# Two graph layers on 64 graphs: tile places from a written table instead of rotating buffers, with the order of work written anew

## The chip, the cores and the metric

The kernel runs on one core of a Trainium2 chip. The core has five engines with a queue each: TensorE (PE, matrix products), VectorE (DVE), ScalarE (ACT), GpSimd (POOL) and SyncE (SP), which here issues all transfers between DRAM and the on-chip memory SBUF. PE writes its results to PSUM, eight banks of 2 KB in each of 128 partitions; DVE and ACT read them there. The metric is the device time in microseconds, the median of several runs.

## The reference

64 graphs of 256 nodes with 512 features go through two layers. All products are in float32.

```python
# x: (64, 256, 512); adj: (64, 256, 256), about 1.6% ones and the diagonal
h = relu(layernorm(x))                              # layer 0: gated attention, 8 heads of 64
q, k, v = h @ Wq.T, h @ Wk.T, h @ Wv.T
scores = where(adj != 0, q_h @ k_h.T / 8, -inf)     # per head, 256 x 256
c = concat_h(softmax(scores) @ v_h)
gate = sigmoid(concat(c, h) @ Wg.T + bg)
x = x + gate * h + (1 - gate) * c

h = relu(layernorm(x))                              # layer 1: GAT
Wh = h @ W                                          # 512 x 512
e = leaky_relu((Wh @ a1)[:, None] + (Wh @ a2)[None, :], 0.2)
att = softmax(where(adj == 0, -1e9, e))
x = x + elu(att @ Wh)
```

## The kernel before

**Tiling.** A graph's 256 tokens lie in two halves of 128 partitions (index `t`). The five large products (`qk`, `v`, `z` for the gate, `wh`, and `po` for the attention of layer 1) are done by a seven-product scheme for 2 x 2 block matrices instead of eight. `product` (lines 377 to 422) makes its steps: seven products on PE, named by a digit (`qk.1`, `v.6`, `wh.3`), which accumulate in three banks `pma`, `pmb`, `pmc`; and sums that empty the banks, `u1`, `u2`, `u3` into small tiles and `c00` to `c11` into the four quarters of the result. `u1` and `c00` are ACT copies (line 409), the others DVE additions (line 405). The sums of operand blocks that the scheme needs are made on POOL: `Sh`, `Sg`, `Sc`, `S1` (`token_sums`, line 375), `Sp` and `Rp` (lines 829 and 839). `wh.6`, for example, reads `S1.1`, which reads `S1.0`, which reads the transposed h of layer 1, `h1T`.

**Half-array work.** Two parts of layer 0 use only half of the PE array for one product. The scores (`sc.0` and `sc.1`, four heads each, line 589) have 64 rows of contraction: tile 64\*128. The weighing of v (`we.00` to `we.11`, line 649) gives 64 rows of output: tile 128\*64. All other products use the whole array, 128\*128.

**One graph's way.** Load x and adj (`load`, `edges`, `mask`); statistics and normalisation (`st0`, `root0`, `nb0`, `nm0`); a transpose by 32 x 32 blocks on DVE (`th`) and through DRAM (`sh` sends, `fh` fetches, four issues each); `qk`, `v`; scores. Then by head group and pair: `max` on DVE takes the masked row minimum of the negated scores out of PSUM and writes them into a tile `e` (line 599); `exp` on ACT with the row sums; `rec`; `scale` on POOL, for one pair on ACT; `turn`, `send`, `fetch` transpose it into `eT`; `we` multiplies with v into `pc`; `cT` copies that out on ACT, `tc`, `sc_c`, `fc` transpose it to c. `z` is the gate's product, followed by `tanh`, `diff`, `plus`, `mix`, `res`. Layer 1 is `st1` to `fh1`, `wh`, `ej` (the row of a2 products), `lo`, `lk`, `gm`, `gx`, `tg`, `sg`, `fg`, `po`, `neg`, `pos`, `xn`, `elu`, `add`, `store`.

**Order.** No scheduler decides the order. `PLAN` (line 23) gives every step of a graph a number; graph g's steps get 48 g added (`ROUND`), all steps of all graphs are sorted by the sum, and each engine's queue gets its steps in that order (lines 921 to 931). So in the middle of the run every 48 units the same sequence stands in each queue, one round, with steps of four or five graphs between each other: at 66 a graph g-1 is weighed where graph g, at 18, has its scores. The numbers are only sort keys; the time comes from the engines. `MOVED` has tables of their own for the first three and last three graphs, `ONCE` the loading of the weights and their sums.

**Memory.** `new` and `bank` (lines 273 to 277) hand out tiles. A pool has a number of buffers, and a new tile takes the place of an older one; the first write waits for the last reader of the tile that was there. There are 15 places of 4 KB for each partition in the pools S (3), qk (2), v, e (5), cT, z (2) and h, 8 places of 2 KB in tmp (5) and U (3), and one pool `ps` of eight banks. The pool e serves the `e`, the turned `eb` and the fetched `eT` tiles of all head pairs.

Of the kernel before, what the change touches and what calls it, by code (L numbers as in the profile page):

```python
# [8 lines left out]
F32 = mybir.dt.float32  # L9
# [14 lines left out]
load@-56.857 st0.0@-50.914 st0.1@-50.386 root0@-38.451 nb0@-30.73 nm0.1@-29.303 nm0.0@-26.84 th.1@-26.684  # L24
th.0@-25.569 sh@-25.308 fh@-18.664 edges@-17.435 Sh.0@-12.146 Sh.1@-9.433 qk.1@-2.883 qk.u1@-2.523 qk.6@-2.39
qk.u2@-2.35 Sh.2@-2.097 qk.7@-1.86 qk.2@-0.28 qk.5@0.348 qk.u3@2.467 Sh.3@2.69 qk.4@3.061 qk.c11@3.306 v.6@6.188
qk.c10@6.582 qk.3@8.941 v.1@10.525 qk.c01@12.52 qk.c00@13.266 v.5@13.583 mask@15.096 v.u1@16.001 v.u2@17.374
sc.0@18.765 v.7@18.861 max.001@19.626 max.000@19.866 v.u3@20.741 exp.001@21.355 max.010@22.095 exp.000@22.339
max.011@22.78 rec.00@22.853 v.c11@22.919 sc.1@23.918 v.3@24.165 scale.000@24.323 max.100@24.331 exp.011@24.947
v.c01@25.495 v.4@26.067 exp.010@27.66 max.110@28.028 max.111@28.261 exp.110@29.517 v.c10@29.519 rec.01@29.796  # L30
scale.001@29.819 scale.011@29.852 scale.010@32.212 turn.000@32.42 turn.001@32.926 exp.111@34.024 max.101@34.103
exp.100@34.466 rec.11@34.651 send.00@35.855 exp.101@36.261 scale.111@36.969 scale.110@37.232 turn.010@39.578
rec.10@42.242 turn.011@43.325 turn.110@43.328 turn.111@45.509 send.11@45.574 scale.100@45.966 scale.101@50.812
send.01@50.911 fetch.00@51.498 turn.101@52.285 Sg.0@52.35 fetch.11@54.685 fetch.01@54.883 turn.100@55.607
v.2@56.007 send.10@58.179 Sg.1@59.157 v.c00@61.854 fetch.10@64.798 we.00@69.417 we.01@69.42 we.11@69.423
we.10@69.426 Sg.3@69.567 Sg.2@69.717 cT.0@70.636 again.0@71.536 cT.1@71.646 Sc.0@75.856 tc.1@76.71 Sc.1@77.286
Sc.2@78.04 z.1@78.088 tc.0@78.815 z.6@79.585 Sc.3@80.277 z.u1@81.33 z.u2@83.091 z.5@83.343 sc_c@83.822
again.1@84.32 z.u2b@88.504 fc@88.967 z.7@89.255 z.u3@89.648 z.2@89.946 z.c11@89.956 z.4@91.345 z.c10@92.468
z.c00@92.495 z.3@93.65 z.c11b@93.91 z.c10b@94.31 tanh.11@94.446 diff.1@94.643 plus.1@94.689 diff.0@95.043
tanh.10@95.277 mix.1@95.529 z.c01@95.688 tanh.00@96.088 tanh.01@96.204 res.1@97.347 st1.1@97.913 mix.0@98.1  # L40
plus.0@98.329 res.0@98.674 st1.0@98.902 root1@100.345 nb1@101.327 nm1.1@102.323 nm1.0@102.364 th1.1@105.631
th1.0@105.724 sh1@112.437 fh1@116.746 wh.1@119.955 S1.2@121.277 S1.0@121.873 wh.u1@122.556 S1.1@123.554
wh.6@123.705 wh.u2@124.211 S1.3@125.364 wh.7@126.289 wh.5@126.586 wh.u3@126.939 wh.c11@128.246 wh.3@128.318
wh.2@129.72 wh.4@130.223 wh.c01@130.405 ej@130.423 Rp.0@130.663 wh.c00@130.978 wh.c10@131.603 lo.0@133.072
lo.1@133.143 lk@134.355 gm@135.48 gx.1@136.043 Rp.2@136.959 gx.0@137.014 tg@138.097 sg@139.813 fg@147.647
Rp.1@149.612 Sp.0@150.903 Sp.1@151.174 Sp.2@152.062 po.1@153.282 at.0@153.282 at.1@153.292 po.u1@153.578
po.6@154.2 gr@155.059 po.u2@155.153 po.7@155.525 po.5@157.176 po.2@157.832 Sp.3@159.316 po.u3@159.476
Rp.3@159.584 po.c11@159.831 po.4@160.018 po.c00@160.144 po.c10@160.279 po.3@160.606 po.c01@161.899 neg.0@162.539
pos.0@166.05 xn.0@166.37 neg.1@168.159 elu.0@168.402 pos.1@169.065 xn.1@169.357 elu.1@171.077 add.0@171.691
add.1@171.977 store.1@176.9 store.0@176.9  # L50
# [3 lines left out]
load@-84.838 st0.0@-70.024 st0.1@-65.46 nb0@-55.71 nm0.0@-52.129 nm0.1@-48.626 th.1@-27.17 Sh.0@-23.333  # L54
Sh.2@-18.64 qk.1@-18.134 qk.u1@-16.548 qk.5@-16.542 Sh.1@-16.358 qk.6@-13.56 qk.u2@-10.263 qk.2@-8.853
edges@-6.428 qk.7@-4.801 Sh.3@-2.103 qk.c00@-1.242 Sg.0@-1.138 Sg.2@-0.021 v.1@0.933 qk.u3@1.907 qk.c11@3.015
mask@3.359 qk.4@3.534 qk.c10@5.054 qk.3@7.14 sc.0@7.575 qk.c01@8.745 v.u1@9.235 max.001@9.244 v.6@9.543
exp.001@9.66 max.000@10.361 max.011@10.992 max.010@12.822 exp.000@13.344 Sg.1@13.537 v.u2@14.154 exp.011@14.257
rec.00@14.845 scale.001@17.841 exp.010@18.278 sc.1@18.944 max.101@19.34 max.100@19.638 v.7@19.923
scale.000@21.044 rec.01@21.889 max.110@22.998 exp.101@23.217 exp.100@23.47 v.5@23.574 exp.110@25.264  # L60
max.111@25.447 exp.111@25.812 turn.000@25.816 v.u3@26.697 turn.001@27.642 v.c11@29.899 scale.011@30.602
send.00@30.717 rec.10@32.367 v.4@33.611 scale.010@33.769 rec.11@36.532 v.2@36.903 turn.011@36.926
scale.111@37.258 turn.010@38.7 scale.110@39.488 v.c10@40.294 turn.111@42.261 turn.110@44.463 v.3@46.303
scale.100@46.341 send.01@46.819 again.0@51.194 turn.100@51.475 send.11@51.955 v.c01@52.024 scale.101@52.096
turn.101@52.671 fetch.00@54.339 send.10@57.895 Sg.3@58.891 fetch.01@61.895 fetch.11@62.369 v.c00@63.445
fetch.10@64.006 we.00@65.406 we.01@69.818 we.11@69.946 we.10@70.749 cT.0@71.689 Sc.2@73.405 cT.1@74.297
tc.0@74.313 tc.1@75.286 Sc.0@75.548 Sc.1@75.875 z.1@76.792 Sc.3@77.055 z.u1@78.295 z.6@83.257 sc_c@83.586
z.2@84.765 z.u2@85.297 z.u2b@85.717 z.5@86.726 fc@87.043 z.7@89.137 z.c00@89.679 z.u3@90.346 z.4@90.632
z.c11@91.163 z.3@91.422 z.c10@91.788 tanh.00@91.811 z.c11b@92.331 z.c10b@92.783 again.1@92.976 tanh.10@93.567
diff.1@93.819 z.c01@94.097 tanh.11@94.321 mix.1@94.45 plus.1@94.957 diff.0@95.286 plus.0@95.672 res.1@95.819  # L70
tanh.01@98.203 mix.0@98.476 st1.1@98.567 res.0@98.604 st1.0@100.036 root1@100.041 nb1@100.805 nm1.0@100.923
nm1.1@101.842 th1.0@102.876 th1.1@104.018 sh1@107.675 fh1@117.875 wh.1@120.728 S1.0@121.866 wh.5@121.891
S1.1@122.669 wh.u1@122.916 wh.6@123.053 wh.u2@123.088 S1.2@123.206 wh.2@123.428 wh.7@123.678 S1.3@124.231
wh.u3@124.694 wh.c11@126.668 wh.3@127.963 wh.c00@128.345 wh.c01@128.818 wh.4@129.098 Rp.0@129.804 ej@130.864
wh.c10@130.987 lo.0@131.977 lo.1@133.072 lk@133.478 gm@134.937 gx.1@135.784 gx.0@136.246 Rp.1@136.759 tg@137.074
sg@138.442 Rp.2@144.617 Rp.3@147.603 fg@148.992 Sp.0@149.583 Sp.2@150.994 Sp.1@151.262 po.1@153.424 gr@153.925
po.5@154.132 po.6@154.327 po.u1@155.598 po.u2@155.847 po.7@156.076 po.2@156.832 po.u3@156.928 po.c11@157.27
Sp.3@157.419 po.c00@158.191 po.4@158.939 po.3@159.535 po.c10@160.717 po.c01@160.77 neg.1@161.785 xn.1@162.021
pos.1@163.675 neg.0@165.715 elu.1@167.679 pos.0@168.736 xn.0@172.28 elu.0@173.244 add.1@175.909 add.0@175.952
store.1@177.279  # L80
""",
    1: """
load@-61.561 st0.0@-61.032 st0.1@-56.795 root0@-47.524 nb0@-45.124 nm0.0@-43.984 edges@-41.428 nm0.1@-41.37
mask@-39.285 th.1@-33.096 Sh.0@-25.932 qk.1@-24.669 Sh.1@-16.944 qk.5@-15.713 qk.6@-7.503 v.1@-4.955 Sh.3@-4.874
qk.u1@2.016 qk.u2@2.143 Sh.2@3.263 v.6@3.676 qk.7@5.202 qk.u3@8.896 qk.c11@8.906 v.5@9.315 qk.2@10.371
qk.3@11.942 qk.4@12.452 v.u1@14.127 qk.c01@15.444 qk.c00@15.51 v.u2@16.052 qk.c10@17.228 sc.0@17.921
max.000@18.683 max.001@19.555 exp.000@20.317 max.011@20.943 v.7@21.367 exp.001@21.574 exp.011@22.73 v.u3@23.043
rec.00@23.155 max.010@23.649 scale.000@23.899 v.c11@24.253 sc.1@25.387 max.100@25.753 exp.010@25.931
max.111@27.027 scale.001@29.653 exp.100@29.833 rec.01@29.997 scale.011@30.559 v.3@30.627 max.110@30.978
max.101@33.527 exp.111@33.754 v.c01@34.528 turn.000@34.546 exp.110@35.663 rec.11@35.816 v.4@36.029  # L90
turn.001@36.721 v.c10@36.772 scale.010@37.194 exp.101@37.491 scale.111@37.617 scale.110@38.488 turn.011@39.034
rec.10@39.144 turn.010@40.349 turn.111@40.581 turn.110@42.691 scale.100@43.52 scale.101@43.628 turn.100@44.378
# [141 lines left out]
def kernel(  # L234
# [25 lines left out]
    def pool(name, bufs, **kw):  # L260
        return ctx.enter_context(tc.tile_pool(name=name, bufs=bufs, **kw))

    const = pool("const", 1)
    st = pool("st", 4)
    kept = pool("kept", 5)
    sb = {tag: pool(tag, bufs) for tag, bufs in {
        "x": 5, "mask": 3, "hT": 3, "S": 3, "qk": 2, "v": 1, "wh": 1, "R": 1, "e": 5,
        "cT": 1, "z": 2, "h": 1, "tmp": 5, "U": 3,
    }.items()}
# [694 lines left out]
```

## Time and profile before

| | us |
|---|---|
| median of 3 runs (3203.18 to 3205.24) | 3203.99 |
| the profiled execution | 3206.93 |
| its span, first to last instruction | 3205.1 |
| PE busy in the span | 3160.6 |
| DVE busy | 2599.1 |
| POOL busy | 2208.9 |
| ACT busy | 1490.4 |
| share of 16 DMA engines, q1 | 71.0% |

In the profile a row of PE is one pass of a matmul; a float32 product takes two, so `ps ... x16` are the eight score products of one step. Names are those of the tiles, written out as out<-in. In a row of the time order the columns are start, duration (both us), engine, source line, operation, tiles, shapes, number of rows merged, and in brackets the idle time before it with what seems to have ended it. PEld is the loading of PE's weights, which runs beside the products. Durations of matmuls overlap, since the next one starts while the one before is still in the array.

### The profile page before, as it was taken

How to read it: one execution, taken by the hardware profiler on the slowest of the kernel's cores; microseconds unless marked ns; L12 is line 12 of the kernel's file. 1: busy time of each engine (PE TensorE's matmuls, PEld its weight loads, DVE VectorE, ACT ScalarE, POOL GpSimd, SP SyncE). 2: the span in 40 equal slices, each digit the busy share in tenths (PEclk: the TensorE clock that was granted, in tenths of full speed). 3: DMA queues.
4: the chain of work that ended last, by engine and by line, in shares of the span. 5: the costliest groups of instructions: out<-in, count | busy, mean ns of one | idle time of the engine just before them, and what ended most of it. 6: DMA issues, size and time to landing. Idle time of an engine off the chain costs nothing.

```text
span 3205.1 us, 62526 instructions
## 1 busy us (share of the span) xinstructions
PE 3160.6 (99%) x19542; PEld 2672.1 (83%) x19542; DVE 2599.1 (81%) x6625; ACT 1490.4 (46%) x4165; POOL 2208.9 (69%) x3006
## 2 busy tenths in 40 slices
PE   9999999999999999999999999999999999999997
PEld 8888888888888888888888888888888888888885
DVE  7887887888888877888888888888887888878885
ACT  4445445454454453544544545445445454454452
POOL 4676676676766766767667667676676676766765
PEclk9999999999999999999999999999999999999998
DMA  7776777777777777767777776677777776767763
GB/s 229 166 200 181 183 194 186 191 188 174 203 182 183 195 186 191 187 174 203 181 183 195 185 193 186 170 207 181 183 195 188 189 187 171 207 179 184 202 159 86
DMA packets 1107162, 593.25 MB, mean 185 GB/s; under 512 B 687632, under 2 KB 1032720, under 8 KB 1106832
## 3 DMA queue, kind: packets, MB, share of 16 engines
q1 hardware_dynamic: 1106832, 589.25, 71.0%
q8 instruction: 158, 2.59, 0.3%
q14 instruction: 172, 1.41, 0.2%
HBM read 306.45 MB, written 282.59 MB: 184 GB/s over the span
## 4 chain that ended last, share of the span: by engine, by line
PE 86%; POOL 7%; issue 3%; DVE 1%; DMA 1%; SPq 0%; ACT 0%; POOLq 0%; DVEq 0%; ACTq 0%
PE pmb_qk L390 10%; PE pmb_z L390 10%; PE pc L649 7%; PE pma_qk L390 7%; PE pmc_qk L390 7%; PE pma_z L390 7%; PE pmc_z L390 7%; PE ps L589 6%; PE pmb_wh L390 6%; POOL S L375 5%; PE pmb_v L390 4%; PE pmc_wh L390 3%; PE pma_v L390 3%; PE pmb_po L390 3%; PE pmc_v L390 2%
## 5 line engine op out<-in xcount | busy, mean ns | idle before, releaser
L625 POOL TENSOR_SCALAR e<-e,rec 128x256 f32<-128x256 f32 x768 | 396.1, 530 | 679.3 <-PE ps L589 632.4
L609 ACT ACTIVATE e<-e,low 128x256 f32<-128x256 f32 x1024 | 510.3, 501 | 199.6 <-DVE low L599 194.5
L599 DVE CUSTOM_DVE_ANT_0 e<-ps,mask 128x256 f32<-128x256 f32 x1024 | 379.9, 412 | 157.3 <-DMA h1T<-there_h 77.0
L460 ACT ACTIVATE h<-x,nb_l,rs_l 128x512 f32<-128x512 f32 x256 | 195.2, 808 | 459.9 <-DMA eT<-there_e 219.5
L631 DVE STREAM_TRANSPOSE eb<-e 128x512 f32<-128x512 f32 x512 | 348.6, 691 | 6.9
L589 PE MATMUL ps<-qk 64*128 64x256 f32 x2048 | 297.4, 395 | 9.9 <-DVE low L599 9.5
L589 PEld LDWEIGHTS ps<-qk 64*128 64x128 f32 x2048 | 198.6, 186 | 102.4 <-DVE low L599 35.3
L649 PE MATMUL pc<-eT,v 128*64 128x256 f32 x2048 | 249.9, 386 | 5.4 <-DMA eT<-there_e 4.4
L649 PEld LDWEIGHTS pc<-eT,v 128*64 128x64 f32 x2048 | 135.7, 136 | 110.6 <-DVE low L599 28.2
L609 ACT ACTIVATION_READ_ACCUMULATOR e<-e,low 128x1 f32 x1024 | 194.9, 190 | 0.0
L702 POOL TENSOR_TENSOR x<-x,c 128x512 f32<-128x512 f32 x128 | 191.3, 1494 | 2.7 <-DMA c<-there_c 2.7
L892 POOL TENSOR_TENSOR x<-x,po 128x512 f32<-128x512 f32 x126 | 185.3, 1472 | 10.7 <-DVE po L884 10.7
L450 POOL TENSOR_TENSOR rs_l<-ve_l,mhalf 128x2 f32<-128x2 f32 (+1 forms) x129 | 91.8, 712 | 129.3 <-DVE ve_l L446 116.6
L439 DVE BATCH_NORM_STATS2 bs_l<-x 128x6 f32<-128x512 f32 x256 | 174.3, 681 | 7.7 <-DMA x<-in_x_dram 3.5
L409 ACT COPY u_qk<-pma_qk 128x512 f32<-128x512 f32 x64 | 37.5, 586 | 298.5 <-PE pma_qk L390 298.4
L707 ACT ACTIVATE z<-z 128x256 f32<-128x256 f32 x256 | 93.4, 412 | 175.9 <-DVE z L405 155.6
L697 POOL TENSOR_TENSOR d<-d,c 128x512 f32<-128x512 f32 x128 | 165.6, 1294 | 3.0 <-DMA c<-there_c 1.6
L468 DVE STREAM_TRANSPOSE h<-h 128x512 f32<-128x512 f32 x248 | 165.3, 684 | 0.3 <-ACT h L460 0.3
L414 POOL TENSOR_TENSOR z<-z,bias 128x256 f32<-128x256 f32 x128 | 93.5, 731 | 88.7 <-DVE z L405 79.7
L405 DVE TENSOR_TENSOR u_po<-pmb_po,u_po 128x256 f32<-128x256 f32 x126 | 52.7, 419 | 113.3 <-ACT u_po L409 102.6
L390 PE MATMUL pmb_wh<-w_t,S 128*128 128x257 f32 x512 | 138.4, 392 | 4.6 <-DVE u_wh L405 0.6
L390 PE MATMUL pma_qk<-hT,wq_sb 128*128 128x128 f32 x1024 | 136.1, 276 | 2.7 <-DVE hT L501 2.7
(173 smaller groups left out, 8987.2 us busy)
## 6 DMA issues: line engine op xcount, KB each, us to landing
there_e<-eb SPq DMA_DIRECT2D x256, 512.0 KB, 3.9
eT<-there_e SPq DMA_DIRECT2D x1024, 128.0 KB, 3.5
there_h<-h SPq DMA_DIRECT2D x496, 128.0 KB, 3.3
there_c<-cb SPq DMA_DIRECT2D x64, 512.0 KB, 4.8
c<-there_c SPq DMA_DIRECT2D x256, 128.0 KB, 5.0
x<-in_x_dram SPq DMA_DIRECT2D x63, 512.0 KB, 6.1
out_dram<-x SPq DMA_DIRECT2D x63, 512.0 KB, 4.1
hT<-there_h SPq DMA_DIRECT2D x248, 128.0 KB, 3.0
```

The lines of the kernel that those rows point to most:

```text
L390: nc.tensor.matmul(s[name, key][(slice(None), *cols)], lhsT, rhs, start=first and i == 0, stop=last and i == len(mms) - 1, skip_group_chec ...
L439: nc.vector.bn_stats(bs, s["x"][:, t, :])
L460: nc.scalar.activation(out, s["x"][:, t, :], AF.Relu, bias=s["nb", layer][:, t:t + 1], scale=s["rs", layer][:, t:t + 1])
L589: nc.tensor.matmul(s["ps", half, jj, i][:, t, :], qk[r:r + DK, 0, jj, t * P:(t + 1) * P], qk[r:r + DK, 1, jj, :], start=True, stop=True,)
L599: nc.vector.tensor_tensor_reduce(e[:, i, t, :], s["ps", half, jj, i][:, t, :], s["mask"][:, t, :], -SCALE, HUGE, ALU.add, ALU.min, accum_o ...
L609: nc.scalar.activation(e, e, AF.Exp, bias=s["low", half][:, jj, i, t:t + 1], scale=-1.0, accum_out=sums[:, jj, i, t:t + 1])
L625: nc.gpsimd.tensor_scalar(e, e, rec, 1.0, ALU.mult, ALU.mult)
L631: nc.vector.transpose(eb[:, :, 4 * i:4 * i + 4, :].rearrange("p b n c -> p n b c"), e)
L649: nc.tensor.matmul(pc[i * DK:(i + 1) * DK, jj, :].rearrange("p (t a c) -> p t a c", t=NT, c=32), s["v"][:, kc, hd * DK:(hd + 1) * DK], s[" ...
L697: nc.gpsimd.tensor_tensor(d, d, s["c"][t], ALU.subtract)
L702: nc.gpsimd.tensor_tensor(xt, xt, s["c"][t], ALU.add)
L892: nc.gpsimd.tensor_tensor(xt, xt, s["pos", t], ALU.add)
```

## The change

Every tile but those of five kinds gets a place by name. `HOME` gives for each kind of tile its place, and where two numbers stand, the first is for graphs with an even number and the second for odd ones; `HOMES` has tables of their own for the first and last three graphs. There are 15 large places (4 KB), 8 medium ones (2 KB) and 8 banks, as many as the pools had. The tiles x, mask, hT, wh and Rp keep rotating buffers. The step tables `PLAN`, `MOVED` and `ONCE` are replaced throughout. In the new `PLAN` the four `we` steps of a graph have numbers that fall between `sc.0` and `sc.1` of the next graph, with no other PE step between these six. No step changes what it computes or the engine it runs on.

Of the tables the diff shows the lines that the prediction speaks of.

```diff
 PLAN = """
...
-qk.c10@6.582 qk.3@8.941 v.1@10.525 qk.c01@12.52 qk.c00@13.266 v.5@13.583 mask@15.096 v.u1@16.001 v.u2@17.374
-sc.0@18.765 v.7@18.861 max.001@19.626 max.000@19.866 v.u3@20.741 exp.001@21.355 max.010@22.095 exp.000@22.339
-max.011@22.78 rec.00@22.853 v.c11@22.919 sc.1@23.918 v.3@24.165 scale.000@24.323 max.100@24.331 exp.011@24.947
...
-v.2@56.007 send.10@58.179 Sg.1@59.157 v.c00@61.854 fetch.10@64.798 we.00@69.417 we.01@69.42 we.11@69.423
-we.10@69.426 Sg.3@69.567 Sg.2@69.717 cT.0@70.636 again.0@71.536 cT.1@71.646 Sc.0@75.856 tc.1@76.71 Sc.1@77.286
...
-th1.0@105.724 sh1@112.437 fh1@116.746 wh.1@119.955 S1.2@121.277 S1.0@121.873 wh.u1@122.556 S1.1@123.554
-wh.6@123.705 wh.u2@124.211 S1.3@125.364 wh.7@126.289 wh.5@126.586 wh.u3@126.939 wh.c11@128.246 wh.3@128.318
...
+qk.c00@2.902 v.6@6.373 qk.c11@6.599 qk.c10@7.236 qk.3@10.925 v.1@13.726 sc.0@13.916 max.000@14.395 v.u1@14.853
+max.010@15.863 max.001@15.981 max.011@16.298 qk.c01@16.63 v.u2@17.05 exp.000@17.735 sc.1@17.987 exp.010@18.004
+v.7@18.092 v.5@18.445 max.100@18.691 max.101@18.934 v.u3@19.508 v.c11@19.513 exp.011@20.27 max.110@20.373
...
+send.10@52.665 fetch.11@55.316 fetch.00@56.632 Sg.0@61.755 fetch.10@62.154 fetch.01@62.554 Sg.1@62.628
+we.10@63.137 we.11@63.14 we.00@63.143 we.01@63.146 cT.1@65.083 cT.0@65.432 Sc.2@65.47 Sg.2@65.68 z.1@68.201
...
+nm1.1@105.297 nm1.0@107.607 th1.1@108.104 th1.0@108.66 sh1@111.487 fh1@113.781 S1.0@117.405 S1.1@117.725
+wh.1@121.42 wh.6@121.622 S1.2@121.67 wh.5@121.818 wh.u1@122.472 wh.u2@122.877 wh.7@123.017 wh.2@123.434
...
+HOME = """
...
+eT_1_1@5/10 e_0_0@13/12 e_0_1@0/13 e_1_0@5/10 e_1_1@1/9 eb_0_0@14/0 eb_0_1@3/6 eb_1_0@2/5 eb_1_1@4/5 eg@6/3
+egT@5/0 h@14/6 h1@2/10 h1T@14/2 neg_0@3/2 neg_1@7/6 pc_0@2/5 pc_1@0 pe@1 pma_po@5 pma_qk@5 pma_v@4/6 pma_wh@5/2
...
+po_0@4 po_1@0/7 ps_0_0_0@5/2 ps_0_0_1@3 ps_0_1_0@7/5 ps_0_1_1@6/4 ps_1_0_0@6/1 ps_1_0_1@7/3 ps_1_1_0@3/2
+ps_1_1_1@0/4 qk_0@9/14 qk_1@4/11 u1_po@3/4 u1_qk@7/2 u1_v@5/2 u1_wh@7/0 u1_z@0/4 u2_po@2/5 u2_qk@2/6 u2_v@3/5
...
-    sb = {tag: pool(tag, bufs) for tag, bufs in {
-        "x": 5, "mask": 3, "hT": 3, "S": 3, "qk": 2, "v": 1, "wh": 1, "R": 1, "e": 5,
-        "cT": 1, "z": 2, "h": 1, "tmp": 5, "U": 3,
-    }.items()}
-    ps = pool("ps", 8, space=bass.MemoryType.PSUM)
+    sb = {tag: pool(tag, bufs) for tag, bufs in {"x": 5, "mask": 3, "hT": 3, "wh": 1, "R": 1}.items()}
+    large, medium = pool("large", 1), pool("medium", 1)
+    ps = pool("ps", 1, space=bass.MemoryType.PSUM)
...
+    homes = {}
+    for number, text in [(None, HOME), *HOMES.items()]:
+        for kind, at in table(text):
+            homes[kind, number if number is None or number >= 0 else B + number] = at.split("/")
+
+    def home(kind, g):
+        of = homes.get((kind, g)) or homes[kind, None]
+        return of[g % len(of)] if g is not None else of[0]
...
-    def new(tag, shape, name, dt=F32):
-        return sb[tag].tile(shape, dt, tag="t", name=name)
+    def new(tag, shape, kind, g, dt=F32):
+        if tag in sb:
+            return sb[tag].tile(shape, dt, tag="t", name=named(kind, g))
+        return {"large": large, "medium": medium}[tag].tile(shape, dt, tag=f"at{home(kind, g)}", name=named(kind, g))
...
-    def bank(shape, name):
-        return ps.tile(shape, F32, tag="t", name=name)
+    def bank(shape, kind, g):
+        return ps.tile(shape, F32, tag=f"at{home(kind, g)}", name=named(kind, g))
...
-        e = lazily(s, ("e", half, jj), lambda: new("e", [P, 2, NT, N], f"e_{g}_{half}_{jj}"))
+        e = lazily(s, ("e", half, jj), lambda: new("large", [P, 2, NT, N], f"e_{half}_{jj}", g))
```

All other calls of `new` and `bank` change in the same way.

## The prediction

> **What bounds the kernel now.** I read the page first, then a window of one round, then TensorE's rows of that round in order of time, then VectorE's rows in the same stretch, then the waits.
>
> ```profile
> PE 3160.6 (99%) x19542; PEld 2672.1 (83%) x19542; DVE 2599.1 (81%) x6625; ACT 1490.4 (46%) x4165; POOL 2208.9 (69%) x3006
> ```
>
> TensorE is busy 99% of the span. The end of a matmul is modelled, though, so I take its cost from the distance between starts.
>
> ```profile
> 1500.00:1549.28 49.28, 49.04 (x306) 41.49 (x305) 40.36 (x104) 23.17 (x65) 34.53 (x48) 1.00 0.70 182
> ```
>
> One round (the same work for the next graph) takes 49.28 us: score starts repeat at that distance. Columns: length, busy time of PE, weight loads, DVE, ACT, POOL, then granted clock 1.00, DMA share. No other engine is near 49.
>
> ```profile
> 1508.07 1.05 PE L390 MATMUL pmb_qk<-Sh,wq_t 128*128 128x128 f32 x8
> 1508.96 1.06 PE L390 MATMUL pmb_qk<-Sh,wk_t 128*128 128x128 f32 x8
> ...
> 1523.08 0.59 PE L390 MATMUL pmc_po<-wh,Sp 128*128 128x256 f32 x2
> 1523.61 2.00 PE L589 MATMUL ps<-qk 64*128 64x256 f32 x16
> 1525.53 1.13 PE L390 MATMUL pmb_v<-wv_t,Sh 128*128 128x256 f32 x4
> 1526.59 3.91 PE L649 MATMUL pc<-eT,v 128*64 128x256 f32 x32
> 1530.44 1.56 PE L589 MATMUL ps<-qk 64*128 64x256 f32 x8
> 1532.16 1.13 PE L589 MATMUL ps<-qk 64*128 64x256 f32 x8 [0.16 <-DVE low L599]
> 1533.23 1.14 PE L390 MATMUL pma_wh<-w_sb,h1T 128*128 128x257 f32 x4
> 1534.20 1.02 PE L390 MATMUL pmc_v<-wv_sb,Sh 128*128 128x256 f32 x4
> 1535.06 1.03 PE L390 MATMUL pmb_v<-wv_t,hT 128*128 128x256 f32 x4
> 1536.15 1.14 PE L390 MATMUL pmb_wh<-w_t,S 128*128 128x257 f32 x4
> 1537.12 1.02 PE L390 MATMUL pma_z<-wgh_sb,hT 128*128 128x256 f32 x4
> ```
>
> Undisturbed rows: 128 columns 0.89/8 = 0.1116 us (8.07 to 8.96), 256 columns 0.86/4 = 0.2165 (34.20 to 35.06), half-array rows 3.85/32 = 0.12 (26.59 to 30.44). A round has 112 rows of the first kind, 126 of the second, 64 of the third and two transposes of 0.11: 12.50 + 27.28 + 7.68 + 0.21 = 47.67 us. So 49.28 - 47.67 = **1.61 us a round is lost on TensorE**, and the rows show where. po to scores, 0.53 for 0.43: 0.09, entering half-array work. The v product between the two half-array pieces, 1.06 for 0.87: 0.20, out and in again. sc.1, 1530.44 to 1533.23 for 1.92: 0.87. wh after it, 0.97 for 0.87: 0.11, out. pmb_v and pmb_wh, 1535.06 to 1537.12 for 1.73: 0.33. An odd 0.04 makes up the rest with rounding.
>
> ```profile
> 1524.67 0.49 DVE L867 TENSOR_SCALAR neg<-po,rec 128x512 f32<-128x512 f32 x1
> 1527.73 0.42 DVE L599 CUSTOM_DVE_ANT_0 e<-ps,mask 128x256 f32<-128x256 f32 x1 [2.57 <-DMA h1T<-there_h]
> ...
> 1531.68 0.42 DVE L599 CUSTOM_DVE_ANT_0 e<-ps,mask 128x256 f32<-128x256 f32 x1
> 1532.03 0.09 DVE L599 DVE_READ_ACCUMULATOR2_ANT low<- 128x1 f32 x1
> ```
>
> This explains the 0.87. The first row maximum could have run soon after sc.0 (1523.61) but starts at 1527.73. The releaser named is a DMA long done; what ended just then is the first quarter of pc (1526.59 + 8 x 0.12 = 1527.55), which reads eT_0_0, and of the five rotating "e" buffers e_0_0 gets the one that eT_0_0 had. So four maxima end only at 1532.03, and the banks of sc.1's second half come free then (its rows restart at 1532.16, released by "low").
>
> ```profile
> PEld pmb_wh L390 <- POOL S L375: 27.3, 58, 0.8
> ```
>
> The 0.33 is wh.6 waiting for POOL's sums of h1T, in 58 rounds. POOL itself stood in its queue behind a scale step until 1532.36.
>
> **The change, part by part.** No instruction is added or removed: every engine issues as many of each kind as before, and the same memory is cut into the same 15 + 8 places and 8 banks. Only order and places move, so all cost is in waits and mode changes.
>
> *One half-array stretch.* TensorE's new order is po.3, v.1, sc.0, we.10, we.11, we.00, we.01, sc.1, v.7. By the rows above one exit and one entry go: 0.20 of 0.40. The Trainium skill speaks against so much: "TensorEngine Tiling (Array Packing)", Key Properties, says that changing the tiling mode drains TensorE. Scores (64\*128) and weighing (128\*64) are different modes, so by the rule there are four changes where five were, and the gain is about 0.10. The nearest rows:
>
> ```profile
> 91.66 1.93 PE ps L589 x16
> 93.59 2.74 PE pc L649 x24
> ```
>
> Here scores pass straight into pc at 0.12 a row, nothing added, and pc into sc.1 (26.59 to 30.44) adds nothing either. I take 0.20; by the rule the total below is 6 us worse.
>
> *Fixed places: the maxima's start.* e_0_0 now gets place 13 (even graphs) or 12 (odd), whose last reader (a turn, or z.3) is done by z.3's end, some 16 us ahead by the count below. The wait for pc is gone. New limits are VectorE's own queue and the banks. The skill's same page, PSUM Bottleneck, warns that packed tiles speed up TensorE and not the evacuation. Here ten bank-sized outputs appear in 7.7 us with 8 banks, so sc.1 must wait for maxima. I walk VectorE's queue with start-to-start times from this trace. It is pinned once a round, by z.c01 waiting for z.3. Count from z.3's last issue. qk.6 (1.79 later, +0.20 for a result to reach VectorE, as 1523.08 to 1523.28 for po<-pmb_po) starts qk.u2 at 1.99. Then qk.u2 0.60, mix.0 and .1 0.90 each, gr 0.10, res 1.0 twice, qk.u3 0.60, st1 2.0, qk.c11 and c10 1.2, st0 2.0, nb1 0.28, three po sums 1.02, th1 1.22, po.c10 0.34, neg.1 0.60, po.c01 0.34: 14.1, so VectorE is free for max.000 at 16.1. TensorE reaches sc.0 at 15.55 and the first scores are there at 16.0. Then four max steps of 0.69, nb0 0.28, elu.1 0.96, qk.c01 0.60: 4.6, done at 20.7. sc.1 needs exactly these (banks, and qk_1 by qk.c01). TensorE asks for it at 15.55 + 1.93 + 3.85 = 21.3. **Slack 0.6 us**, so the 0.87 goes to 0. If the cover is gone, VectorE later by t costs t - 0.6 a round. The last banks hang on ACT: pc_0's copy (0.57) after we.01, about 0.20 + 0.57 after 21.3 = 22.1, against 21.3 + 0.96 = 22.3 for sc.1's second half. Nothing, but close.
>
> *POOL's sums earlier.* S1.0 and S1.1 now stand ahead of all scale steps, behind Sc.2, Sg.2, add.1 and Sc.0 (0.70, 0.69, 1.24, 0.70). cT.0 releases that run at 22.1 on the same count, so S1.0 could start at 25.4. Its data come later: th1.0 ends at 14.8, sh1's four issues of 0.6 and 3.3 to land give 20.5, fh1's four and 3.4 give 26.3. S1.0 and S1.1 (0.70 each) are done at 27.7. wh.6 comes after sc.1, v.7, v.5, z.1, v.4, v.3, wh.1: 23.2 + 0.11 + 6.06 = 29.4. Slack 1.7 us, so the 0.33 goes; h1T later by t costs t - 1.7.
>
> *Transfers.* SP's 52 issues of about 0.6 us are all kept. The tight pair is turn.100, send.10, fetch.10, we.10. turn.100 ends near z.3's end (0); send.10 stands behind fg's four issues, 1.5; it lands 3.9 later (page) at 5.4; fetch.10, behind fetch.11 and fetch.00 (4.8 of issues), is issued by 9.3 and lands 3.5 later, at 12.8; fetch.01 at 15.2. we.10 runs at 17.5, we.01 at 20.4. Slack 4.7 us. load waits for the store of three graphs earlier, with only send.00 and later steps behind it; those have the same slack. Everything else moved has more.
>
> *Head and tail.* Six graphs have orders of their own, all remade. From sc.0 of graph 3 (141.4) to sc.0 of graph 63 (3099.9) are 60 rounds, 2958.6 us, 49.31 each. Outside lie 246.5, of which some 200 is matmul work; the same work stands on either side of these marks in the new order. Of the other 46 I allow 10 either way and take 0.
>
> *Sum.* New round 47.67 + 0.20 + 0.03 for small waits = 47.90. 60 x (49.31 - 47.90) = 84.6. The profiled execution took 3206.9 (span 3205.1), the median of the runs is 3204.0: 3204.0 - 84.6 = 3119.4, **3120**.
>
> **Rivals.**
> - *The stall only moves* (B). VectorE's mix and res rows run from 0.64 to 1.4 us when POOL works beside them, and qk.c01 now stands behind four maxima where it stood long before them; 0.6 us is soon used up. With half of 0.87 + 0.33 left: 60 x 0.6 = 36 more, about 3157. Against: VectorE is 81% busy and pinned anew each round, so lateness doesn't pile up.
> - *The change does nothing* (C). The mode changes save 0.1 and a full new wait replaces the two old ones: 60 x 0.1 = 6, 3198, or level. For it: the rotating buffers may have hidden a third limit. Against: no engine but TensorE fills a round.
> - *Slower* (D). we.10 stands right behind sc.0, so a late fetch.10 stops TensorE with sc.1 and all else behind it; now (before the change) eT_1_0 comes last of four, at 1529.5, and the other three give it cover. DMA is 70% busy and a round is 3% shorter. It must come 4.7 us later than walked to cost anything and 6.1 to cancel the gain of 1.41; at 6.7 us the round is 49.9, and 60 x 0.6 = 36 more than before make 3240.
>
> **How the numbers follow.** Main case 0.72, at 3120, own range 3106 to 3140 (below: 60 x 47.67 + 246.5 = 3107 with no loss at all, less 10 for head and tail; above: 0.3 us of waits left a round). B 0.20, 3140 to 3190. C 0.03. D 0.05. The range leaves out a little below and the upper part of B with C and D: 3104 to 3165. A measurement of this kernel tells 0.2%, 6 us, from no change. Faster is the main case, B and nothing of D: 0.92; same 0.03; slower 0.05.
>
> **What would show it.** Scores, 32 rows of pc and scores in one unbroken run of about 7.7 us; the first maximum within 0.6 us of sc.0 and no pc in front of it; no "low" as releaser of ps; no POOL S before pmb_wh; a round of 47.9. Wrong if ps waits for the qk product or cT, if pc waits for eT, or if the stretch has 0.1 us at each of its inner seams.

## The result and the profile after

The changed kernel takes **3176.42 us** (median; 3175.03 to 3177.40) against 3204.60 us (3203.18 to 3205.24) for the kernel before on the same chip: a ratio of 0.9912, 95% interval 0.9895 to 0.9930. It is faster by 28 us, 0.9%, with the runs of each kernel within 2.4 us of each other. The forecast was 3120, 85 us faster, range 3104 to 3165: right direction, wrong size. From sc.0 of graph 3 to sc.0 of graph 63 (140.2 to 3072.8), 60 rounds took 48.88 us each where they took 49.31; 60 x 0.43 = 26 us. The profiled executions' spans differ by 32 us (3205.1 and 3173.2), so 26 of the gain lie in the rounds and 6 before and behind them.

The engines' busy times on the page of the changed kernel, which tell as little as before:

```profile
PE 3097.0 (98%) x19542; PEld 2673.1 (84%) x19542; DVE 2607.4 (82%) x6625; ACT 1506.8 (47%) x4165; POOL 2176.8 (69%) x3006
```

One round of it, from the window view (length, then busy time of PE, weight loads, DVE, ACT, POOL, granted clock, DMA share):

```profile
1507.09:1555.95 48.86, 47.98 (x306) 41.58 (x305) 40.25 (x104) 23.60 (x66) 34.04 (x47) 1.00 0.73 189
```

48.86 against 47.67 of matmul work: 1.2 us a round are still lost, where the forecast left 0.23. TensorE's rows in order of time, first around the scores, then around the qk products:

```profile
1507.09 2.00 PE L656 MATMUL ps<-qk 64*128 64x256 f32 x16
1509.01 3.67 PE L716 MATMUL pc<-eT,v 128*64 128x256 f32 x32
1512.62 2.00 PE L656 MATMUL ps<-qk 64*128 64x256 f32 x16
1514.55 1.13 PE L457 MATMUL pmb_v<-wv_t,Sh 128*128 128x256 f32 x4
1515.52 1.03 PE L457 MATMUL pmc_v<-wv_sb,Sh 128*128 128x256 f32 x4
...
1544.54 1.06 PE L457 MATMUL pmc_qk<-Sh,wq_sb 128*128 128x128 f32 x8
1545.43 1.06 PE L457 MATMUL pmc_qk<-Sh,wk_sb 128*128 128x128 f32 x8
1547.36 1.16 PE L457 MATMUL pmb_qk<-hT,wq_t 128*128 128x128 f32 x8 [0.88 <-DVE u_qk L472]
1548.36 1.06 PE L457 MATMUL pmb_qk<-hT,wk_t 128*128 128x128 f32 x8
```

The half-array work is one stretch of 7.46 us (1507.09 to 1514.55), and sc.1 follows pc without a gap: the 0.87 is gone. But qk.4, the product that goes on in bank pmb_qk, starts at 1547.36 where 1545.43 + 0.89 = 1546.32 would do: **1.04 us**, and 0.10 more to start again (1548.36 - 1547.36 = 1.00 for 0.89). It comes in nearly every round, as TensorE's list of waits says (releaser, us in total, times, longest). First the changed kernel, then the kernel before:

```profile
PE pmb_qk L457 <- DVE u_qk L472: 51.8, 62, 0.9
```

```profile
PE ps L589 <- DVE low L599: 9.5, 58, 0.2
...
PE pmb_qk L390 <- DVE u_qk L405: 1.5, 1, 1.5
```

The new list has no "low" before ps and no "POOL S" before pmb_wh, which had 9.5 and 27.3 us in the list before. VectorE's and GpSimd's rows of the same stretch:

```profile
1541.22 0.69 DVE L472 TENSOR_TENSOR u_qk<-pmb_qk,u_qk 128x512 f32<-128x512 f32 x1 [0.82 <-PE pmb_qk L457]
1541.83 1.48 DVE L778 SCALAR_TENSOR_TENSOR d<-z,d 128x512 f32<-128x512 f32 x1
1543.23 0.15 DVE L864 RECIPROCAL rec<-sums 128x2 f32<-128x2 f32 x1
1543.30 1.14 DVE L778 SCALAR_TENSOR_TENSOR d<-z,d 128x512 f32<-128x512 f32 x1
1544.36 2.34 DVE L782 SCALAR_TENSOR_TENSOR x<-d,x 128x512 f32<-128x512 f32 x2
1546.63 0.68 DVE L472 TENSOR_TENSOR u_qk<-pmb_qk,u_qk 128x512 f32<-128x512 f32 x1
```

```profile
1540.07 2.68 POOL L769 TENSOR_TENSOR x<-x,c 128x512 f32<-128x512 f32 x2
1542.72 1.17 POOL L906 TENSOR_TENSOR Rp<-Rp,wh 128x256 f32<-128x256 f32 x1
1543.85 1.17 POOL L906 TENSOR_TENSOR wh<-wh 128x256 f32<-128x256 f32 x1
1544.98 1.17 POOL L442 TENSOR_TENSOR Sh<-hT,Sh 128x256 f32<-128x256 f32 x1
```

The second u_qk is qk.u3. It must read pmb_qk before qk.4 may write there, and in the new order it stands behind mix, gr, mix and both res. Those four took 1.1 to 1.5 us each, and GpSimd's rows beside them 1.17, while u_qk with GpSimd at work beside it took 0.69.

The new order also took away cover. Before, product 3 of z stood between qk's products 6 and 7. Rows of TensorE and of VectorE before (z.3 and qk.4; qk.u2 and qk.u3):

```profile
1506.34 1.03 PE L390 MATMUL pmc_z<-wgh_sb,Sg 128*128 128x256 f32 x4
...
1513.42 1.06 PE L390 MATMUL pmb_qk<-hT,wq_t 128*128 128x128 f32 x8
```

```profile
1506.61 0.68 DVE L405 TENSOR_TENSOR u_qk<-pmb_qk,u_qk 128x512 f32<-128x512 f32 x1
...
1511.65 0.68 DVE L405 TENSOR_TENSOR u_qk<-pmb_qk,u_qk 128x512 f32<-128x512 f32 x1
```

TensorE asked for qk.4 7.08 us after qk.6 had been issued, and qk.u3 had ended 1.09 us earlier, at 1512.33. Now z.3 stands ahead of qk.6, and TensorE asks after 5.36 us (1540.96 to 1546.32), while VectorE needs 6.09 us from qk.u2's start to qk.u3's end where it needed 5.72. So in these two rounds 1.72 us of cover are gone on TensorE, against 0.37 us more on VectorE. No run put z.3 back.

### The profile page after: what moved, and what is told of

It is laid out like the page before. It is cut to its first block, busy times and chain, and to the rows that moved or that the text cites. A ratio compares the mean times of both kernels' runs of the same rounds, so it can differ in the third digit from the quotient of the medians.

```text
span 3173.2 us, 61830 instructions
## 1 busy us (share of the span) xinstructions
PE 3097.0 (98%) x19542; PEld 2673.1 (84%) x19542; DVE 2607.4 (82%) x6625; ACT 1506.8 (47%) x4165; POOL 2176.8 (69%) x3006
## 4 chain that ended last, share of the span: by engine, by line
PE 78%; DVE 11%; issue 6%; DMA 5%; SPq 1%; POOL 0%; ACT 0%; DVEq 0%; POOLq 0%; ACTq 0%
PE pmb_z L457 8%; PE ps L656 8%; PE pc L716 7%; PE pmb_qk L457 6%; PE pma_z L457 5%; PE pmb_v L457 5%; PE pmb_wh L457 5%; PE pmc_z L457 5%; PE pmc_qk L457 4%; PE pma_qk L457 3%; PE pma_wh L457 3%; DMA there_e<-eb 3%; PE pma_v L457 3%; PE pmc_wh L457 3%; PE pmc_v L457 3%
## 5 line engine op out<-in xcount | busy, mean ns | idle before, releaser
L442 POOL TENSOR_TENSOR Sc<-cT 128x256 f32<-128x256 f32 x128 | 104.3, 815 | 506.0 <-ACT cT L725 506.0
L692 POOL TENSOR_SCALAR e<-e,rec 128x256 f32<-128x256 f32 x768 | 359.4, 485 | 18.6 <-DVE rec L683 15.4
L656 PE MATMUL ps<-qk 64*128 64x256 f32 x2048 | 255.7, 389 | 0.0
L656 PEld LDWEIGHTS ps<-qk 64*128 64x128 f32 x2048 | 187.9, 186 | 61.6 <-issue 23.2
L716 PE MATMUL pc<-eT,v 128*64 128x256 f32 x2048 | 236.7, 383 | 0.8 <-DMA eT<-there_e 0.8
L959 POOL TENSOR_TENSOR x<-x,po 128x512 f32<-128x512 f32 x126 | 160.3, 1272 | 32.1 <-DVE po L951 18.6
L476 ACT COPY u_po<-pma_po 128x256 f32<-128x256 f32 x63 | 23.4, 372 | 330.7 <-PE pma_po L457 321.6
L769 POOL TENSOR_TENSOR x<-x,c 128x512 f32<-128x512 f32 x128 | 172.2, 1363 | 1.5 <-DMA c<-there_c 1.1
L778 DVE SCALAR_TENSOR_TENSOR d<-z,d 128x512 f32<-128x512 f32 x128 | 163.5, 1280 | 0.9 <-POOL x L769 0.6
L782 DVE SCALAR_TENSOR_TENSOR x<-d,x 128x512 f32<-128x512 f32 x128 | 145.7, 1175 | 0.4
```

Source lines behind the costliest of these rows:

```text
L656: nc.tensor.matmul(s["ps", half, jj, i][:, t, :], qk[r:r + DK, 0, jj, t * P:(t + 1) * P], qk[r:r + DK, 1, jj, :], start=True, stop=True,)
L692: nc.gpsimd.tensor_scalar(e, e, rec, 1.0, ALU.mult, ALU.mult)
L716: nc.tensor.matmul(pc[i * DK:(i + 1) * DK, jj, :].rearrange("p (t a c) -> p t a c", t=NT, c=32), s["v"][:, kc, hd * DK:(hd + 1) * DK], s[" ...
L769: nc.gpsimd.tensor_tensor(xt, xt, s["c"][t], ALU.add)
```

## The experiments

All are edits of the table `PLAN` of the changed kernel; a step's number sets its place in every queue. No computation is left out. Theory 1 is that VectorE's order makes qk.u3 late; its refinement (1b) that GpSimd's work beside mix and res makes it late; the rival (2) that TensorE's loss only moves from one VectorE step to the next, whatever is freed.

### qk.u3 earlier, and later

```diff
-qk.u3@1.668
+qk.u3@0.95
```

> One step of the changed kernel is moved: qk.u3 stands between the two res steps in VectorE's queue, not behind both. Theory 1 (order): product 4 of qk waits 1.04 us a round, and 0.10 to start again, because qk.u3, which empties its bank, stands behind mix, gr and res. Then qk.u3 ends about 0.5 to 1.1 us earlier, the wait falls to 0 to 0.2 us, the round goes from 48.86 to 47.7 to 47.9 us, and the time to 3105 to 3125 us. Theory 2 (the wait only moves): the next wait of TensorE, sc.1 for the maxima whose slack is about 0.2 us, takes what is freed, and the time stays over 3150 us. Theory 3 (qk.u3 isn't what product 4 waits for): 3173 to 3180 us, no change.

Measured: 3153.35 us (ratio to before 0.9837, interval 0.9822 to 0.9851), 23 us under the changed kernel. Theory 1 has the mechanism and theory 2 the time, with another step than sc.1. The wait before qk.4 fell from 51.8 us to 2.7 (5 times), but a new one took 20.1:

```profile
PE pmb_po L457 <- DVE u_po L472: 20.1, 54, 0.6
```

It is po's product 7, which goes on in bank pmb_po, waiting for po.u2 (the last expectation under "mask, then Sh.3, out of the way" calls it product 2), with some 0.1 us to start again. VectorE's window from qk.u2 to the last po sum (length, busy time) shows why:

```profile
1482.24:1496.65 14.41, 14.10 (x28) 1.00 0.95 226
```

VectorE has hardly a pause for 14.4 us. An earlier qk.u3 lets TensorE run 1 us ahead to the next product that needs a VectorE sum, and this sum stands behind the same amount of work. The other direction:

```diff
-qk.u3@1.668 qk.4@1.724
+qk.u3@4.0 qk.4@4.1
```

> The other way: qk.u3 goes behind one more step of VectorE, st1.1 (about 0.8 us). Theory 1: the wait before product 4 grows by these 0.8 us a round, some 49 us in all: 3215 to 3235 us, slower than the kernel before the change. Theory 3 (qk.u3 isn't what sets it): 3173 to 3185 us.

Measured: 3227.74 us (1.0066, 1.0049 to 1.0083), 51 us over the changed kernel where 49 were expected, and the same line of the list of waits doubled:

```profile
PE pmb_qk L457 <- DVE u_qk L472: 103.4, 61, 1.9
```

So qk.u3 is what product 4 waits for, and one VectorE step of 0.8 us in front of it costs 0.8 us a round, enough to undo the whole gain.

### GpSimd's work away from mix and res

```diff
-Rp.1@144.203 ... Rp.2@145.991
+Rp.1@141.811 ... Rp.2@141.812
```

> The order on VectorE is that of the changed kernel; two operations of GpSimd (Rp.1, Rp.2) are moved ahead, into its idle time before the last copy of z, so that they no longer run beside mix and res. Theory 1a (the order alone makes qk.u3 late): mix and res keep 1.2 to 1.5 us, the time stays at 3173 to 3180 us. Theory 1b (the order leaves no slack, and GpSimd's work beside mix and res stretches them from about 0.65 us to 1.2 to 1.5 us): the two res steps shrink to some 1.5 us together, qk.u3 ends 0.7 to 0.9 us earlier, the wait falls to 0.2 to 0.4 us and the time to 3120 to 3140 us.

Measured: 3151.99 us (0.9833, 0.9818 to 0.9849). VectorE's order is unchanged, so order alone (1a) falls; but 3120 to 3140 was missed too. In most rounds the expectation held: both res together 1.28 instead of 2.34, and no wait worth naming. In other rounds something new stood in front, and made TensorE wait with qk's product 7 instead of 4:

```profile
PE pmb_qk L457 <- DVE u_qk L472: 36.4, 27, 2.1
```

VectorE's and then GpSimd's rows of such a round of this kernel:

```profile
1384.90 3.95 DVE L586 TENSOR_SCALAR mask<-adj 128x512 bf16<-128x512 int32 x1
1388.77 0.68 DVE L472 TENSOR_TENSOR u_qk<-pmb_qk,u_qk 128x512 f32<-128x512 f32 x1
1389.37 0.68 DVE L778 SCALAR_TENSOR_TENSOR d<-z,d 128x512 f32<-128x512 f32 x1
```

```profile
1384.16 1.27 POOL L764 TENSOR_TENSOR d<-d,c 128x512 f32<-128x512 f32 x1
1385.38 2.50 POOL L769 TENSOR_TENSOR x<-x,c 128x512 f32<-128x512 f32 x2
1387.84 0.72 POOL L442 TENSOR_TENSOR Sh<-hT,Sh 128x256 f32<-128x256 f32 x1
```

The mask step, 0.68 us in the other rounds, took 3.95: it began in the middle of GpSimd's d and ended 0.29 us after the last of four GpSimd instructions in a row. In 20 of 64 graphs it took over 1.6 us, in none of the changed kernel's. (The execution that was traced, 3159.49 us, is the slowest of four from 3147.19 on; how many graphs it hit in the others is not known.) Afterwards, with GpSimd idle, mix took 0.68. With both moves together the loss was the same:

> Both moves of the first two together. If qk.u3's place alone cures the wait, this is as the first, 3105 to 3125 us, within 0.2 per cent of it. If the first leaves a rest of wait because mix and the first res are stretched, this one takes it: 5 to 15 us under the first. Theory 2 (the wait moves to sc.1): both stay over 3150 us.

Measured: 3157.32 us (0.9846, 0.9832 to 0.9861), within 0.2% of the first, and over 3150 as theory 2 has it, but not for its reason: ps waits for nothing, and pmb_qk waits 31.8 us in 22 places, mask being long in 17 graphs. qk.u3's place adds nothing while mask stops the queue in front of it.

### mask, then Sh.3, out of the way

```diff
-mask@-0.706
+mask@-11.0
```

> The kernel with Rp.1 and Rp.2 moved, and VectorE's mask moved too, 10.3 us of the plan earlier, to before u_z, where GpSimd is idle for 1.7 us. Theory (one at a time): mask and GpSimd's operations on SBUF exclude each other, and in 20 of the 64 graphs mask waited through GpSimd's whole unbroken run (3.9 us and more instead of 0.68), which made qk.u2 late by 1.8 us. Then mask takes 0.4 to 0.7 us everywhere, the 33 us of waits before qk's second products go, and the time is 3112 to 3124 us. Rival (mask's long rows are no cause, the second products wait for something else): 3145 to 3160 us, as without this move.

Measured, on top of the moved Rp steps: 3133.07 us (0.9770, 0.9754 to 0.9786). mask's median fell to 0.42 us. The time came down 19 us, but 9 short of the expectation. In part of the rounds the first mix now met the same fate: d took 2.46 us in rounds like that at 1375.7: it started 0.04 us after a GpSimd x did and ended 0.54 us after the Sh behind that x. So Sh.3 was moved as well:

```diff
-Sh.3@2.277
+Sh.3@4.6
```

> As the last, and Sh.3 on GpSimd goes behind Sp.0 and Sp.1, so that nothing but the two plus operations stands beside mix and res. Theory (one at a time): the second mix falls from 1.14 to 0.68 us, qk.u3 ends 0.4 to 0.5 us earlier, the rest of the wait before product 4 (about 0.08 us a round) goes: 2 to 8 us under the last, 3108 to 3120 us. Rival (VectorE's mix is slow of itself, not for GpSimd's sake): mix stays at 1.14 us, and the time within 3 us of the last.

Measured: **3119.36 us** (3119.07 to 3120.38; ratio 0.9730, 0.9715 to 0.9744), faster than both kernels and 14 us under the last, more than expected. VectorE's rows of one round of it, GpSimd idle from 1515.70 to 1518.70:

```profile
1514.35 0.69 DVE L472 TENSOR_TENSOR u_qk<-pmb_qk,u_qk 128x512 f32<-128x512 f32 x1 [1.43 <-PE pmb_qk L457]
1514.96 1.29 DVE L778 SCALAR_TENSOR_TENSOR d<-z,d 128x512 f32<-128x512 f32 x1
1516.17 0.15 DVE L864 RECIPROCAL rec<-sums 128x2 f32<-128x2 f32 x1
1516.25 0.67 DVE L778 SCALAR_TENSOR_TENSOR d<-z,d 128x512 f32<-128x512 f32 x1
1516.84 1.28 DVE L782 SCALAR_TENSOR_TENSOR x<-d,x 128x512 f32<-128x512 f32 x2
1518.04 0.68 DVE L472 TENSOR_TENSOR u_qk<-pmb_qk,u_qk 128x512 f32<-128x512 f32 x1
```

qk.u3 ends 4.37 us after qk.u2's start; in the changed kernel it was 6.09. The instructions and their order on VectorE are the same but for mask, which left the place in front of qk.u2; VectorE had 0.82 us to spare there in the changed kernel, so that this alone moves nothing. The first mix, which still starts beside GpSimd's x, took 1.47 us on average. The same 14.41 us as in the first experiment's window (columns as in the round's window above), and a whole round:

```profile
1514.35:1528.76 14.41, 14.41 (x108) 13.25 (x108) 13.24 (x28) 3.78 (x8) 7.20 (x12) 1.00 0.93 235
```

```profile
1528.04:1575.82 47.78, 47.78 (x305) 41.47 (x304) 38.68 (x104) 23.34 (x66) 32.58 (x47) 1.00 0.76 193
```

VectorE's busy time in the stretch is 13.24 us, where that window had 14.10, and TensorE never stops. pmb_qk waits for u_qk 5.6 us, 6 times, in the whole kernel, in the first and last graphs, which have orders of their own. Sixty rounds take 47.96 each, and 60 x (48.88 - 47.96) = 55 of the 57 us gained. Theory 1b holds, and theory 2 only as long as VectorE is full.

> The last version of the repair (Rp, mask and Sh.3 moved away from mix and res) with qk.u3 between the two res steps as well. In the repair without it, six graphs still wait before product 4, 5.6 us in all; an earlier qk.u3 should take these away: 3112 to 3118 us. If VectorE's stretch from qk.u2 to the pos steps has no room left, as where qk.u3 alone was moved, product 2 of po waits instead, and the time stays at 3117 to 3125 us.

This adds qk.u3@0.95 to the last. Measured: 3119.73 us (0.9735, 0.9719 to 0.9752), the six waits still there (5.9 us): no gain. The time is that of the expectation's second reading, but the reason is that the waits left lie in graphs that this move doesn't touch.

### The one stretch of half-array work

```diff
-sc.1@17.987
+sc.1@18.3
```

> The changed kernel with one part undone: sc.1 goes behind v's product 7, so that the half-array work of a round is in two stretches again. Theory of the prediction (leaving and entering half-array work costs 0.10 us each): one exit and one entry more, 0.20 us a round, 12 us in all: 3186 to 3190 us. By the page's rule as the prediction read it (a seam between row and column tiles drains too, so that two of three seams are there anyhow): 0.10 us a round, 3181 to 3184 us. If sc.1's slack for the maxima is not the 0.2 us of the trace but below nothing, sc.1 also gains by standing later, and the time stays at 3174 to 3180 us.

Measured: 3234.09 us (1.0085, 1.0070 to 1.0101), 58 us over the changed kernel; all three expectations missed. The rows of TensorE say that most of it is no mode change:

```profile
1538.42 3.67 PE L716 MATMUL pc<-eT,v 128*64 128x256 f32 x32
1542.27 1.13 PE L457 MATMUL pmb_v<-wv_t,Sh 128*128 128x256 f32 x4 [0.17 <-DVE u_v L472]
1543.33 2.00 PE L656 MATMUL ps<-qk 64*128 64x256 f32 x16
1545.26 1.13 PE L457 MATMUL pmc_v<-wv_sb,Sh 128*128 128x256 f32 x4
1546.62 1.13 PE L457 MATMUL pma_z<-wgh_sb,hT 128*128 128x256 f32 x4 [0.23 <-DVE low L666]
```

v's product 7, called 1.93 us earlier, waits for v.u2; z.1 waits for a bank that the maxima free, and one of wh's products for a sum that is late now. Each costs 0.23 us a round on average over the sixty rounds, with the restart, and the mode change proper 1543.33 - 1542.27 = 1.06 for 0.87, 0.19. Together they are nearly all of 49.81 - 48.88 = 0.93. A cleaner cut, on the 3119 us version:

```diff
-v.1@13.726
+v.1@14.0
```

> The repair (Rp, mask, Sh.3 moved), with v's product 1 between sc.0 and we.10, where the kernel before had v's product 7: two stretches of half-array work a round, with sc.1 still right behind the last we. The prediction's size for the one stretch: 0.20 us a round, 12 us: 3129 to 3134 us. The page's rule as the prediction read it: 0.10 us a round, 3124 to 3127 us. What the run with sc.1 behind v's product 7 lost between pc, v and sc.1: 0.43 us a round, 3142 to 3148 us.

Measured: 3152.28 us (0.9837, 0.9822 to 0.9851), 33 us over the version without it. Again it is more than any expectation, and again not for the mode change:

```profile
1543.23 2.00 PE L656 MATMUL ps<-qk 64*128 64x256 f32 x16 [0.49 <-ACT po L476]
1545.15 1.13 PE L457 MATMUL pma_v<-wv_sb,hT 128*128 128x256 f32 x4
1546.21 3.67 PE L716 MATMUL pc<-eT,v 128*64 128x256 f32 x32
1549.82 2.00 PE L656 MATMUL ps<-qk 64*128 64x256 f32 x16
```

v between costs 1546.21 - 1545.15 = 1.06 for 0.87, **0.19**, in each round: 11 us. sc.0, 0.87 us earlier, has to wait for ScalarE's copy of po, another 0.27 a round on average and 0.07 to start again, and the rest is small waits at po's products. (The 0.43 quoted in the expectation held 0.24 of waiting for v.u2.)

## Why the prediction was wrong, step by step

**What bounds the kernel**: right. TensorE sets the time; every gain and loss of the runs is a wait on it.

**One stretch, 0.20 us a round**: the size right, the reasoning not, so in part by luck. A v product set between halves costs 0.19 in both runs that put one there. But the prediction let scores pass into pc with "nothing added", and that is wrong. Within one kind of half-array work two rows start every 216 ns in the trace, so that 16 rows take 1.73 us and 32 rows 3.46; in the changed kernel scores take 1509.01 - 1507.09 = 1.92, pc 3.61 and sc.1 1.93. From scores to pc two neighbouring starts lie 313 ns and then 267 ns apart, 0.15 us more than twice 216, and from pc to sc.1 it is 0.20, as much as entering or leaving half-array work costs (0.20 each, the last row before the change and the first behind it together). The 0.12 us a row of the prediction held these seams already. So its last sign of being wrong, 0.1 us at each inner seam, did come. The rule of the Trainium skill ("TensorEngine Tiling (Array Packing)", Key Properties), that a change of tiling mode drains TensorE, agrees with these rows: four changes where there were five, at 0.15 to 0.20 us each, and one less is worth the 0.19. What was wrong was to price it at 0.10. Before, pc had a restart of 0.24 us between its two halves, at a wait on a semaphore; it is gone, and makes the stretch 0.23 us a round better than predicted. Why it went wasn't tried.

**The maxima's start, the 0.87**: its end came as predicted, by less margin. The first maximum starts 1.16 us after sc.0 (1508.25), released by ps, not by pc. I had written 0.6 us. The slack of sc.1 was about 0.2 us (qk.c01 ends near 1512.4, TensorE asks at 1512.62), not 0.6.

**The walk of VectorE's queue: here it failed**, in the sentence "Then qk.u2 0.60, mix.0 and .1 0.90 each, gr 0.10, res 1.0 twice, qk.u3 0.60". Two things. First, I walked the queue for one customer, sc.1, and never asked who waits for each step on the way. By the walk's own numbers qk.u3 is done at 1.99 + 0.60 + 1.80 + 0.10 + 2.00 + 0.60 = 7.09 after z.3's last issue, and TensorE asks for qk.4 after four products of 1.785: 7.14. A slack of 0.05 us stood there unread, with z.3 no longer between to cover more. Second, the 0.90 and 1.0 are means of the old neighbourhood. In the new one VectorE's four steps stand beside Rp, wh and Sh of GpSimd, and mix with gr took 2.53 and res 2.27 where 1.90 and 2.00 were walked: 0.90 us more. The Trainium skill has the rule that would have warned: "SBUF — State Buffer", Who interferes with whom, says that a VectorE instruction with two inputs in SBUF and a GpSimd instruction that reads SBUF exclude each other. This case agrees: mix and res (two SBUF inputs) take 0.67 alone and 1.1 to 1.5 beside GpSimd, whose 0.72 becomes 1.17; u_qk (one input in PSUM) keeps 0.69 beside it. With 1.1 to 1.5 for each of the four steps in the walk, the wait is there. It measured 1.14 us with its restart in the round shown, and 1.08 on average over the sixty rounds, 65 us in all. pc's lost restart gives back 60 x 0.23 = 14, and other small waits take some 8: 59, as the rounds say, 60 x (48.88 - 47.90). Head and tail give back 6, and the profiled executions differ from the medians by 4 in all, which leaves the 57 between 3120 and 3176.

**POOL's sums earlier, the 0.33**: right, no such wait is left. **Transfers**: right; pc waits for eT once, 0.8 us. **Head and tail at 0**: within the 10 us allowed; outside the sixty rounds lie 240.6 us (3173.2 - 2932.6) where 246.5 lay.

**The rivals**: B ("the stall only moves ... mix and res rows run from 0.64 to 1.4 us when POOL works beside them") had the mechanism, but looked for the stall at sc.1 and sized it at 0.6 us a round; it came at qk.4 with 1.08. Its range, 3140 to 3190, held the result. With Rp, mask and Sh.3 moved the round is 47.96 us and the time 3119, close to the forecast (47.90, 3120) for a round without this wait. That they agree so well is luck: the half-array stretch came out some 0.24 us better than walked, and small waits on TensorE cost some 0.3 instead of 0.03. C and D did not happen.

**Left open.** The change's two halves, places and orders, weren't tried apart, nor was z.3 put back between qk's products 6 and 7. That the old 0.87 came from e_0_0 following eT_0_0 in a rotating buffer is therefore argued from the traces alone. What decides whether a VectorE step lets one GpSimd instruction pass or several is open too.

## What to carry to other kernels

When orders are rewritten, walk each queue once for every step's own customers, the other engine's next product included, and not only for the stall that one hopes to remove. Price a VectorE step by who works beside it in the new order: two inputs in SBUF beside a run of GpSimd instructions cost 1.1 to 1.5 us here instead of 0.67, and pauses in GpSimd's queue are worth as much as shorter steps. A repair that only reorders a full queue hands the wait to the next customer (here 23 us won of the 57 that were there); taking contention out of the stretch won them.

## What was not expected of the hardware

A VectorE step can be held by a whole run of GpSimd instructions, not just by the one in progress: mask 3.95 us, through d, x, x and Sh. In the rounds of that trace where it started with 0.40 us or less of d left, it got through at the end of d (0.68 us, and the next x took 1.45 instead of 1.27); in those with 0.48 to 0.74 us left it waited for the first pause. So a shift of 0.1 us between the queues made TensorE stand idle for 1.4 to 2.1 us in a third of the graphs. It is no clean threshold: three masks at the start and end of the run, with 0.86 to 1.23 us left, got through as well. mask also has one input in SBUF only, so the two-input rule above does not cover it; why it and GpSimd exclude each other is not shown here.
